# A spectral convolution with its head: the inverse transform along the rows of even layers in 32x32 tiles, and another order of work in a pair of chunks

## The chip, the cores and the metric

The kernel runs on one core of one Trainium2 chip. The metric is the device time of one execution in microseconds, the median of three runs. TensorE is called PE here, its loads of weights PEld, VectorE DVE, ScalarE ACT, GpSimd POOL, and SyncE, which only issues transfers, SP.

## The reference, cut to what matters

Eight images of 8 channels and 256 x 256 pixels. Each goes through four spectral layers (a transform of the plane, a mix of the 24 x 12 lowest frequencies, the transform back, plus a 1x1 convolution), then through a head (fc1, swish, fc2), and at the end a dilation:

```python
h = gconv1x1(concat([gn(x), grid]), fc0_w, fc0_b)          # 4 groups of 10 channels
for i in range(4):
    h1 = spectral_conv(h, sp_w1[i], sp_w2[i])               # rfft2, mix of modes, irfft2
    h2 = gconv1x1(h, w_w[i], w_b[i])
    h = h1 + h2
    if i < 3:
        h = gswish(h, betas[i])
h = gswish(gconv1x1(h, fc1_w, fc1_b), betas[3])             # 4 groups of 128 channels
x = x + gconv1x1(h, fc2_w, fc2_b)
x = x + dilate3x3(gn(x))                                    # maximum over 3 x 3 windows
```

## The kernel before

All data is fp32. Image by image, the kernel runs the four layers; the head of the image before is cut into 128 steps, which are strewn among the layers' work, and the dilation of the image before that follows in small pieces (`tail`) beside some of the steps. PE, DVE and ACT each take their instructions in the order in which the program gives them. All PSUM tiles come from one pool of four slots, each of two banks:

```python
def ps_z(name):
    return ps.tile([128, 2, 512], F32, tag="z", bufs=4, name=name)
def ps_a(name):
    return ps_z(name)[:, 0, :]
```

A layer consists of these parts. After the mix, `p_f` folds the spectrum to real sums; its result is copied to `fz`, in which the 32 values of a channel (`k`) lie on 32 columns and those of the four partition parts `q` on their own columns and partitions:

```python
p = ps_a(f"p_f_{b}_{l}")
for slot in range(2):
    for n, (table, part_of) in enumerate(((0, slot), (1 + slot, 1 - slot))):
        for q in range(4):
            mm(p[part(q), 120 * slot : 120 * slot + 120], fold[part(q), table, :],
               f[part(q), part_of]..., start=n == 0, stop=n == 1)
...
for q in range(4):
    copy(q, fz[part(q), :, :, 6 * q : 6 * q + 6]..., p[part(q), :240]...)
```

The inverse transform along the rows, `p_g`, in an even layer one matmul over the full array for each of the ten channels, then a copy to `zt`:

```python
for o in range(0, WID, 2):                      # WID = 10
    p = ps_z(f"p_g_{b}_{l}_{o}")
    for u in range(2):
        if l % 2 == 0:
            mm(p[:, u, : NBLK * CS * NQ], fz[:, o + u].rearrange("p g k -> p (g k)"),
               rowg.rearrange("p n j r -> p (n j r)"), start=True, stop=True)    # 264 columns
        else:
            ...                                  # 16 matmuls of 66 columns per channel
    for u in range(2):
        copy(u, dst, src)
    yield 0.7
```

Then eleven chunks of pixels. `burst(c)` computes the new state of a chunk (lines 476/479 and 482 on PE, two ACT instructions, line 488); `turn(c)` transposes it on DVE (line 430); `transform(k)` is the forward transform along the columns of a pair of chunks (line 447 on PE, then one half copied by DVE and the other by ACT); `gather(k)` adds it up (line 461 on PE, a DVE copy). Their order in a layer that is not the last:

```python
yield "even"                                     # a step, if needed, so that the next has an even number
for c in range(0, NCH, 2):                       # NCH = 11
    k = c // 2
    yield (1,)                                   # one step of the head, and a piece of dilation
    burst(c)
    yield (1,)
    if k > 0:
        transform(k - 1)
    late = [i for i in range(c, min(c + 2, NCH)) if i > c or c + 1 < NCH and not alone[0]]
    if c not in late:
        turn(c)
    if c + 1 < NCH:
        burst(c + 1)
    if k > 0:
        gather(k - 1)
    for i in late:
        turn(i)
out_["sw"] = [load_sw(l + 1, 0), load_sw(l + 1, 1)]
yield 1.5                                        # 1.5 shares of steps (a share is about 0.9 step)
transform(k)
yield 2
gather(k)
yield 0.5
```

`alone[0]` holds for image 0 only, beside which no head runs. A step `n` of the head is `first(n)` (fc1: line 629 on PE, two slots, two ACT instructions of line 631); after an odd step follows `second(n - 3)` (fc2 of two steps: line 651 on PE, one slot, one DVE addition of line 656):

```python
for n in range(STEPS):                           # STEPS = 128
    ...
    first(n)
    if n % 2 == 1 and n > 2:
        second(n - 3)
    yield
second(STEPS - 2)
```

Of the kernel before, what the change touches and what calls it, by code (L numbers as in the profile page):

```python
# [10 lines left out]
F32 = mybir.dt.float32  # L11
# [7 lines left out]
HW = 256  # L19
NPIX = HW * HW  # L20
G = 4
# [15 lines left out]
PIX = 2 * HW  # L37
DR = 2
STEPS = 128
SIDE = 4.2  # L40


@with_exitstack
def fno_dilate_kernel(ctx: ExitStack, tc: tile.TileContext, a: dict, out: bass.AP):
# [16 lines left out]
    def part(i):  # L61
        return slice(32 * i, 32 * i + 32)
# [30 lines left out]
    xe = load("xe", (128, 6, G, 5), nc.sync)  # L93
    wext = const.tile([128, G, WID, 5], F32, tag="c_wext", name="c_wext")
    nc.sync.dma_start(wext.rearrange("p g o j -> p (g o j)"), a["wext"].partition_broadcast(128))
    cz = load("cz", (32, 5, WID, G))
    fold = load("fold", (128, 3, 32))
    rowg = load("rowg", (128, NBLK, NQ, CS))
    binv = load("binv", (128, HW))
    eh_f = load("eh_f", (128, 3, NBLK, 32))  # L100
# [70 lines left out]
    for l in range(3):  # L171
# [4 lines left out]
    nc.vector.tensor_tensor(cz[0:1, 0], cz[0:1, 0], cv[0:1], ALU.add)  # L176
    nc.sync.dma_start(cz[25:26, 0], cv[1:2])
    nc.sync.dma_start(cz[0:1, 4], cv[2:3])
    nc.vector.tensor_tensor(
        wt, wt, io.rearrange("p (l g) -> p l g", l=4).unsqueeze(3).to_broadcast([128, 4, G, 32]), ALU.mult,  # L180
    )
# [8 lines left out]
    def copy(i, dst, src):  # L190
        if alone[0] and i % 2:
            nc.scalar.activation(dst, src, AF.Identity)  # L192
        else:
            nc.vector.tensor_copy(dst, src)  # L194
# [157 lines left out]
    def mix(b, l, out_):  # L352

        s = [sb.tile([128, 3, G, 2, WID], F32, tag=f"S{i}", bufs=1, name=f"S{i}_{b}_{l}") for i in range(2)]
        bt, sw = out_["bt"], out_["sw"]
        for k in range(3):
            for k2 in range(2):
                pr = turned[:, 2, 1024 * k2 : 1024 * k2 + 800].rearrange("p (g m i) -> p g m i", g=G, i=WID)
                nc.vector.tensor_tensor(  # L359
                    pr, sw[k], bt[:, k2, k].unsqueeze(2).to_broadcast([128, G, 2 * WID, WID]), ALU.mult)  # L360
                yield 0.7
                nc.vector.tensor_reduce(  # L362
                    s[k2][:, k].rearrange("p g s o -> p (g s o)"),
                    pr.rearrange("p g m i -> p (g m) i"), AX.X, ALU.add,
                )
                if k == 0 and k2 == 1:
                    sw.append(load_sw(l, 2))
                yield 0.7
        f = sb.tile([128, 2, 3, G, WID], F32, tag="F", bufs=1, name=f"F_{b}_{l}")
        nc.vector.tensor_tensor(f[:, 0], s[0][:, :, :, 0, :], s[1][:, :, :, 1, :], ALU.subtract)  # L370
        nc.vector.tensor_tensor(f[:, 1], s[0][:, :, :, 1, :], s[1][:, :, :, 0, :], ALU.add)
        yield 0.5

        p = ps_a(f"p_f_{b}_{l}")
        for slot in range(2):
            for n, (table, part_of) in enumerate(((0, slot), (1 + slot, 1 - slot))):
                for q in range(4):
                    mm(p[part(q), 120 * slot : 120 * slot + 120], fold[part(q), table, :],
                       f[part(q), part_of].rearrange("p k g o -> p (k g o)"), start=n == 0, stop=n == 1)
        nc.vector.tensor_copy(fz[0:32, :, :, 24], cz[:, l])  # L380
        if l == 0:
            mr = out_["mr"]
            d = sb.tile([128, 1], F32, tag="d", name=f"dm_{b}")
            nc.vector.tensor_tensor(d, mr[:, 0:1], mr[:, 1:2], ALU.mult)
            mm(p[0:1, 240 : 240 + WID * G], d, wm.rearrange("p o g -> p (o g)"), start=True, stop=True)
            nc.vector.tensor_tensor(
                fz[0:1, :, :, 24], fz[0:1, :, :, 24],
                p[0:1, 240 : 240 + WID * G].rearrange("p (o g) -> p o g", o=WID), ALU.add)
        if l < 2:
            nc.vector.tensor_copy(fz[0:32, :, :, 25], cz[:, 4 if l == 0 else 3])  # L390
        for q in range(4):
            dst = fz[part(q), :, :, 6 * q : 6 * q + 6].rearrange("p o g k -> p k g o")
            src = p[part(q), :240].rearrange("p (k g o) -> p k g o", g=G, o=WID)
            copy(q, dst, src)
        yield 2.5

    def rows_of(b, l):

        zv = zt[:, :, :, : NBLK * WID].rearrange("p r f (n o) -> p o n r f", n=NBLK)
        for o in range(0, WID, 2):  # L400
            p = ps_z(f"p_g_{b}_{l}_{o}")
            for u in range(2):
                if l % 2 == 0:
                    mm(p[:, u, : NBLK * CS * NQ], fz[:, o + u].rearrange("p g k -> p (g k)"),  # L404
                       rowg.rearrange("p n j r -> p (n j r)"), start=True, stop=True)
                else:
                    for g in range(G):
                        for j in range(NQ):
                            mm(p[part(j), u, NBLK * CS * g : NBLK * CS * (g + 1)], fz[:, o + u, g, :],  # L409
                               rowg[:, :, j, :], start=True, stop=True)  # L410
            for u in range(2):
                src = p[:, u, : NBLK * CS * NQ]
                if l % 2 == 0:
                    dst = zv[:, o + u].rearrange("p n r f -> p n f r")
                    src = src.rearrange("p (n f r) -> p n f r", n=NBLK, r=CS)
                else:
                    dst = zv[:, o + u].rearrange("p n r f -> p f n r")
                    src = src.rearrange("p (f n r) -> p f n r", f=NQ, n=NBLK)
                copy(u, dst, src)
            yield 0.7  # L420


    def layer(b, l, out_, stored, side):
        group_in_f = l % 2 == 1

        def turn(c):

            dst = turned[:, c % 3].rearrange("p (s f x) -> p f s x", s=2, f=NQ)
            for i in range(2):
                nc.vector.transpose(  # L430
                    dst[:, 2 * i : 2 * i + 2], h[:, c, 2 * i : 2 * i + 2].rearrange("p f (s x) -> p f s x", s=2))
# [67 lines left out]
        if l == 0:  # L499
# [1 line left out]
                read_x(c)  # L501
            wcn = sb.tile([128, 32], F32, tag="wcn", bufs=1, name=f"wcn_{b}")
            nc.vector.tensor_scalar(wcn, wc, out_["mr"][:, 1:2], None, ALU.mult)
        yield "even"
        if l == 3:
            room = 0.0
            for c in range(NCH):
                yield (1,)
                burst(c)
                room += SIDE  # L510
                while room > 0.0:
                    room -= next(side, SIDE)
                yield (1,)
            return
        for c in range(0, NCH, 2):
            k = c // 2
            yield (1,)
            burst(c)
            yield (1,)
            if k > 0:  # L520
                transform(k - 1)

            late = [i for i in range(c, min(c + 2, NCH)) if i > c or c + 1 < NCH and not alone[0]]
            if c not in late:
                turn(c)
            if c + 1 < NCH:
                burst(c + 1)
            if k > 0:
                gather(k - 1)
            for i in late:  # L530
                turn(i)
        out_["sw"] = [load_sw(l + 1, 0), load_sw(l + 1, 1)]
        yield 1.5
        transform(k)
        yield 2
        gather(k)
        yield 0.5

    def start(b, out_):
        if b < n_img:  # L540
# [68 lines left out]
    def head(b, stored, stats):  # L609
# [6 lines left out]
        def load_state(k):  # L616

            if k < NQ * NCH:
                j, c = k // NCH, k % NCH
                hs[k] = sb.tile([128, PIX], F32, tag="hs", bufs=4, name=f"hs_{b}_{k}")  # L620
                nc.sync.dma_start(hs[k], stored[c][:, PIX * j : PIX * (j + 1)])
# [47 lines left out]
        for n in range(STEPS):  # L669
            if n % 32 % NBLK == 0:  # L670
                load_state(n // 32 * NCH + n % 32 // NBLK + 2)
            first(n)
            if n % 2 == 1 and n > 2:
                second(n - 3)
            yield
        second(STEPS - 2)


    def dilate(b, stats):
# [5 lines left out]
        for r in range(0, 16, DR):  # L685
# [12 lines left out]
            yield  # L698
            nc.vector.tensor_tensor(m, m, yin[:, :, 2 : HW + 2], ALU.max)
            yield  # L700
            o = sb.tile([128, DR, HW], F32, tag="o", bufs=1, name=f"o_{b}_{r}")
            nc.vector.tensor_tensor(o, m[:, 0:DR], m[:, 1 : DR + 1], ALU.max)
            nc.vector.tensor_tensor(o, o, m[:, 2 : DR + 2], ALU.max)
            yield

# [83 lines left out]
def _tables():  # L789
# [50 lines left out]
    for j, v in enumerate(planes):  # L840
# [9 lines left out]
    edge[:, 2], edge[:, 3] = np.where(top, PAD, -BIG), np.where(bottom, PAD, -BIG)  # L850
    tables = {
        "fw": fw, "fw8": fw8, "stack": np.tile(np.eye(32), (4, 1)), "eh0": eh0, "eh_f": eh_f.reshape(128, 3, NBLK, 32),
        "rowg": rowg.reshape(128, NBLK, NQ, CS),
        "fold": fold.reshape(128, 3, 32), "binv": binv.reshape(128, HW),
        "xe": xe.reshape(128, 6, G, 5), "grp": grp, "edge": edge,
    }
    return {k: np.ascontiguousarray(v, f32) for k, v in tables.items()}
# [66 lines left out]
```

## Time and profile before

| | before |
|---|---|
| median of 3 runs | 4137.09 us (4132.44 to 4141.43) |
| span of the profiled run | 4130.5 us, mean granted PE clock 0.973 |
| PE busy | 3709.2 us |
| ACT busy | 2841.6 us |
| DVE busy | 2526.0 us |
| p_g of even layers on PE (line 404) | 320 records, 90.4 us |
| p_g of odd layers on PE (line 409) | 5120 records, 88.0 us |
| p_f on PE (line 378) | 1024 records, 37.4 us |

Two records of the trace stand for one fp32 matmul of the program: 160 calls of line 404 give 320. A line of groups or of the timeline names the engine, the source line, the operation, the tile written and those read, the shape, and the count; "32\*128" with a matmul is the part of the array that its weights fill (rows x columns). "Idle before" is the time for which the engine did nothing just before, with the instruction that ended this wait. In the slices of the span, each digit is the busy share in tenths of one fortieth.

### The profile page before, as it was taken

How to read it: one execution, taken by the hardware profiler on the slowest of the kernel's cores; microseconds unless marked ns; L12 is line 12 of the kernel's file. 1: busy time of each engine (PE TensorE's matmuls, PEld its weight loads, DVE VectorE, ACT ScalarE, POOL GpSimd, SP SyncE). 2: the span in 40 equal slices, each digit the busy share in tenths (PEclk: the TensorE clock that was granted, in tenths of full speed). 3: DMA queues.
4: the chain of work that ended last, by engine and by line, in shares of the span. 5: the costliest groups of instructions: out<-in, count | busy, mean ns of one | idle time of the engine just before them, and what ended most of it. 6: DMA issues, size and time to landing. Idle time of an engine off the chain costs nothing.

```text
span 4130.5 us, 118618 instructions
## 1 busy us (share of the span) xinstructions
PE 3709.2 (90%) x53530; PEld 1483.6 (36%) x53530; DVE 2526.0 (61%) x3535; ACT 2841.6 (69%) x2991; POOL 119.8 (3%) x202
## 2 busy tenths in 40 slices
PE   5666999999999999999999999999999999999997
PEld 2333333333333333333333333333333333333222
DVE  6665655556666566765666666665666656663533
ACT  3334767776667766776766776777676776678887
POOL 1000000000000000000000000000000000000000
PEclk8878999999999999999999999999999999999999
DMA  2005111331115311252122611134111432115311
GB/s 83 14 14 186 50 30 46 133 118 57 57 49 181 91 56 57 77 187 55 58 59 85 195 43 52 54 128 150 56 51 51 163 106 64 55 49 190 94 49 48
DMA packets 113984, 345.05 MB, mean 84 GB/s; under 512 B 15768, under 2 KB 18392, under 8 KB 98056
## 3 DMA queue, kind: packets, MB, share of 16 engines
q1 hardware_dynamic: 95288, 276.33, 21.6%
q0 software_dynamic: 18192, 61.13, 4.5%
q8 instruction: 422, 6.91, 0.7%
q14 instruction: 82, 0.67, 0.1%
HBM read 213.40 MB, written 123.74 MB: 82 GB/s over the span
## 4 chain that ended last, share of the span: by engine, by line
PE 74%; ACT 11%; DVE 11%; issue 3%; DMA 1%; POOL 0%; DVEq 0%; SPq 0%; POOLq 0%; ACTq 0%
PE p_fc L651 22%; PE p_fc L629 17%; PE p_z L482 8%; PE p_d L447 7%; PE p_z L479 7%; ACT act L631 5%; ACT h L488 4%; DVE turned L430 3%; PE p_b L332 2%; PE p_u L461 2%; PE p_g L409 2%; PE p_z L476 2%; PE p_g L404 2%; ACT h L490 2%; DVE fz L194 1%
## 5 line engine op out<-in xcount | busy, mean ns | idle before, releaser
L631 ACT ACTIVATE act<-p_fc 128x1024 f32<-128x1024 f32 x2048 | 1961.5, 1027 | 604.1 <-PE p_fc L629 592.5
L629 PE MATMUL p_fc<-hs,c_w 32*128 32x512 f32 x8192 | 1204.6, 629 | 30.1 <-DVE fz L194 12.8
L651 PE MATMUL p_fc<-act,c_w 128*32 128x512 f32 x8192 | 992.5, 602 | 86.0 <-ACT act L631 43.6
L656 DVE TENSOR_TENSOR y<-p_fc,y 128x512 f32<-128x512 f32 x392 | 270.4, 690 | 651.0 <-PE p_fc L651 649.2
L488 ACT ACTIVATE h<-p_z 128x1024 f32<-128x1024 f32 x528 | 511.8, 1021 | 211.6 <-PE p_z L482 211.5
L629 PEld LDWEIGHTS p_fc<-hs,c_w 32*128 32x128 f32 x8192 | 423.6, 185 | 572.5 <-ACT act L631 251.9
L430 DVE STREAM_TRANSPOSE turned<-h 128x1024 f32<-128x1024 f32 x528 | 612.6, 1213 | 14.5 <-ACT h L488 14.5
L651 PEld LDWEIGHTS p_fc<-act,c_w 128*32 128x32 f32 x8192 | 215.0, 109 | 812.5 <-issue 349.7
L482 PE MATMUL p_z<-c_binv,zt 32*128 32x256 f32 x5632 | 406.8, 401 | 0.6 <-ACT zt L192 0.6
L482 PEld LDWEIGHTS p_z<-c_binv,zt 32*128 32x128 f32 x5632 | 259.7, 184 | 301.5 <-issue 293.3
L479 PE MATMUL p_z<-h,c_wt 32*32 32x512 f32 x8448 | 355.2, 600 | 4.2 <-ACT h L488 3.5
L447 PE MATMUL p_d<-turned,c_fw 32*32 32x480 f32 (+1 forms) x9216 | 312.7, 549 | 37.9 <-DVE turned L430 36.4
L198 ACT ACTIVATE turned<-p_d 128x960 f32<-128x960 f32 x144 | 130.3, 905 | 249.6 <-PE p_d L447 249.6
L200 DVE COPY turned<-p_d 128x960 f32<-128x960 f32 x144 | 154.6, 1074 | 147.3 <-PE p_d L447 145.0
L194 DVE COPY zt<-p_g 128x264 f32<-128x264 f32 x300 | 156.0, 615 | 86.7 <-PE p_g L404 46.3
L490 ACT ACTIVATE h<-p_z,c_bias 128x1024 f32<-128x1024 f32 x176 | 186.6, 1111 | 26.1 <-PE p_z L482 25.7
L447 PEld LDWEIGHTS p_d<-turned,c_fw 32*32 32x32 f32 x9216 | 121.0, 104 | 227.8 <-issue 98.6
L362 DVE TENSOR_REDUCE S<-turned 128x80 f32<-128x800 f32 x192 | 188.9, 984 | 5.2
L359 DVE TENSOR_TENSOR turned<-t,B 128x800 f32<-128x800 f32 x192 | 188.4, 981 | 1.2 <-DMA t<-in_spw 1.0
L323 DVE STREAM_TRANSPOSE turned<-zt 128x960 f32<-128x960 f32 x96 | 174.8, 1864 | 0.8
L461 PE MATMUL p_u<-turned,c_stack 128*32 128x480 f32 (+1 forms) x1152 | 137.4, 548 | 36.3 <-DVE turned L200 36.3
L479 PEld LDWEIGHTS p_z<-h,c_wt 32*32 32x32 f32 x8448 | 97.3, 103 | 190.0 <-ACT h L488 69.1
(169 smaller groups left out, 1957.0 us busy)
## 6 DMA issues: line engine op xcount, KB each, us to landing
stored<-h SPq DMA_DIRECT2D x88, 1024.0 KB
hs<-stored SPq DMA_DIRECT2D x352, 256.0 KB
t<-in_spw SPq DMA_DIRECT2D x96, 400.0 KB
yin<-y_rows POOLq DMA_DIRECT2D x56, 512.0 KB, 5.0
h<-in_xp SPq DMA_DIRECT2D x352, 48.0 KB
turned<-in_x SPq DMA_DIRECT2D x16, 1024.0 KB
y<-in_x SPq DMA_DIRECT2D x56, 256.0 KB
y_rows<-y POOLq DMA_DIRECT2D x56, 256.0 KB, 2.3
```

The lines of the kernel that those rows point to most:

```text
L194: nc.vector.tensor_copy(dst, src)
L430: nc.vector.transpose(dst[:, 2 * i : 2 * i + 2], h[:, c, 2 * i : 2 * i + 2].rearrange("p f (s x) -> p f s x", s=2))
L447: mm(pair[q // 2][part(v % 4), q % 2, : 240 * n], fw8[part(q), v, :], t[part(q), :, :, v, : NBLK * WID], start=v < 4, stop=v >= 4)
L461: mm(p[part(g), : 240 * n], stack, m, start=True, stop=True)
L479: mm(o, wt[part(q), l, g, :], h[part(q), c, f, :], start=True, stop=False)
L482: mm(pair[q // 2][:, q % 2, HW * s : HW * (s + 1)], zt[part(q), 2 * c + s].rearrange("p f o -> p (f o)"), binv[part(q), :], start=False, s ...
L488: nc.scalar.activation(dst, pair[i], AF.Silu)
L490: nc.scalar.activation(dst, pair[i], AF.Identity, bias=bias3)
L629: mm(pair[g // 2][:, g % 2, :], w1[part(g), blk, :], hs[k][part(g), :], start=True, stop=True)
L631: nc.scalar.activation(act[:, 2 * i : 2 * i + 2, :], pair[i], AF.Silu)
L651: mm(acc[part(g), :], w2[:, g, 15 - rb - i : 47 - rb - i], act[:, g, :], start=i == 0, stop=i == 1)
L656: nc.vector.tensor_tensor(y, sums, y, ALU.add)
```

## The change

Two things change. The first is the inverse transform of even layers. The fold's table is four times as wide (its 32 columns repeated four times), so that `p_f` writes four copies of the spectrum, one on each 32 partitions; `fz` holds all four. Then a matmul of 32 rows and 32 columns suffices for one group of one channel, and the four channels of a block use the four row parts of the array and the four groups its column parts: 16 small matmuls take the place of four large ones. Odd layers go on using all 128 rows, which now add up four equal copies; so the table `rowg` is divided by 4, and in even layers `fz` is multiplied by 4. The second is the order: in a pair of chunks, of the steps beside it, at the end of a layer, and in `head`, where fc2 now stands ahead of fc1 of the next even step. Besides, the dilation writes its second maximum in place.

```diff
-        p = ps_a(f"p_f_{b}_{l}")
+        pair = [ps_z(f"p_f_{b}_{l}_{i}") for i in range(2)]
+        p = [pair[q // 2][:, q % 2, :] for q in range(4)]
...
-                    mm(p[part(q), 120 * slot : 120 * slot + 120], fold[part(q), table, :],
+                    mm(p[q][:, 120 * slot : 120 * slot + 120], fold[part(q), table, :],
...
-        nc.vector.tensor_copy(fz[0:32, :, :, 24], cz[:, l])
+        factor = 4.0 if l % 2 == 0 else 1.0
+        nc.vector.tensor_copy(fz[:, :, :, 24], cz[:, l])
         if l == 0:
...                                              # one small addition becomes four, on 1 partition each
         for q in range(4):
-            dst = fz[part(q), :, :, 6 * q : 6 * q + 6].rearrange("p o g k -> p k g o")
-            src = p[part(q), :240].rearrange("p (k g o) -> p k g o", g=G, o=WID)
-            copy(q, dst, src)
+            dst = fz[:, :, :, 6 * q : 6 * q + 6].rearrange("p o g k -> p k g o")
+            src = p[q][:, :240].rearrange("p (k g o) -> p k g o", g=G, o=WID)
+            ...                                  # the same copy, times factor
...
-        for o in range(0, WID, 2):
-            p = ps_z(f"p_g_{b}_{l}_{o}")
-            for u in range(2):
-                if l % 2 == 0:
-                    mm(p[:, u, : NBLK * CS * NQ], fz[:, o + u].rearrange("p g k -> p (g k)"), ...)
+        size = 2 if l % 2 else 4
+        for o in range(0, WID, size):
+            n = min(size, WID - o)
+            p = [ps_z(f"p_g_{b}_{l}_{o}_{i}") for i in range((n + 1) // 2)]
+            for u in range(n):
+                for g in range(G):
+                    if l % 2 == 0:
+                        mm(p[u // 2][part(g), u % 2, : NBLK * CS * NQ], fz[part(u), o + u, g, :], rows[part(u)],
+                           start=True, stop=True)
+                        continue
...
-            yield 0.7
+            yield 0.35 * n
...
-        yield "even"
         if l == 3:
+            yield "odd"
             for c in range(NCH):
-                yield (1,)
                 burst(c)
...                                              # (the transform of the next image's x, in pieces)
-                yield (1,)
+                yield (LAST,)                    # LAST = 2
             return
-        for c in range(0, NCH, 2):
...                                              # (the loop shown above)
+        yield "even"
+        for c in range(NCH):
+            k = c // 2
+            if c % 2 == 0:
+                burst(c)
+                yield (1,)
+                turn(c)
+                if k > 0:
+                    transform(k - 1)
+            else:
+                burst(c)
+                if k > 0:
+                    gather(k - 1)
+                yield (1,)
+                turn(c)
         out_["sw"] = [load_sw(l + 1, 0), load_sw(l + 1, 1)]
-        yield 1.5
+        yield 1
+        gather(k - 1)
         transform(k)
         yield 2
         gather(k)
-        yield 0.5
+        yield 1
...
+            if n % 2 == 0 and n > 3:
+                second(n - 4)
             first(n)
-            if n % 2 == 1 and n > 2:
-                second(n - 3)
             yield
+        second(STEPS - 4)
         second(STEPS - 2)
...
-            o = sb.tile([128, DR, HW], F32, tag="o", bufs=1, name=f"o_{b}_{r}")
-            nc.vector.tensor_tensor(o, m[:, 0:DR], m[:, 1 : DR + 1], ALU.max)
+            o = m[:, 0:DR]
+            nc.vector.tensor_tensor(o, o, m[:, 1 : DR + 1], ALU.max)
```

Three more transfers and three multiplications at the start of the program make the copies of the constant part (`cz`) and its factor of 4.

More of the change, by code (lines that the diff above doesn't have):

```diff
@@ L39 @@
 STEPS = 128
+LAST = 2
 SIDE = 4.2
@@ L95, in fno_dilate_kernel @@
     nc.sync.dma_start(wext.rearrange("p g o j -> p (g o j)"), a["wext"].partition_broadcast(128))
-    cz = load("cz", (32, 5, WID, G))
-    fold = load("fold", (128, 3, 32))
+    cz = const.tile([128, 5, WID, G], F32, tag="c_cz", name="c_cz")
+    nc.gpsimd.dma_start(cz[0:32], a["cz"])
+    fold = load("fold", (128, 3, 128))
     rowg = load("rowg", (128, NBLK, NQ, CS))
@@ L178, in fno_dilate_kernel @@
     nc.sync.dma_start(cz[0:1, 4], cv[2:3])
+    for l in (0, 2, 4):
+        nc.vector.tensor_scalar(cz[0:32, l], cz[0:32, l], 4.0, None, ALU.mult)
+    for q in range(1, 4):
+        nc.sync.dma_start(cz[part(q)], cz[0:32])
     nc.vector.tensor_tensor(
@@ L383, in mix @@
             d = sb.tile([128, 1], F32, tag="d", name=f"dm_{b}")
[L384 to L388, printed above, removed]
+            nc.vector.scalar_tensor_tensor(d, mr[:, 0:1], factor, mr[:, 1:2], ALU.mult, ALU.mult)
+            for q in range(4):
+                mm(p[0][32 * q : 32 * q + 1, 240 : 240 + WID * G], d, wm.rearrange("p o g -> p (o g)"),
+                   start=True, stop=True)
+            for q in range(4):
+                row = slice(32 * q, 32 * q + 1)
+                nc.vector.tensor_tensor(
+                    fz[row, :, :, 24], fz[row, :, :, 24],
+                    p[0][row, 240 : 240 + WID * G].rearrange("p (o g) -> p o g", o=WID), ALU.add)
         if l < 2:
-            nc.vector.tensor_copy(fz[0:32, :, :, 25], cz[:, 4 if l == 0 else 3])
+            nc.vector.tensor_copy(fz[:, :, :, 25], cz[:, 4 if l == 0 else 3])
         for q in range(4):
-            dst = fz[part(q), :, :, 6 * q : 6 * q + 6].rearrange("p o g k -> p k g o")
-            src = p[part(q), :240].rearrange("p (k g o) -> p k g o", g=G, o=WID)
-            copy(q, dst, src)
+            dst = fz[:, :, :, 6 * q : 6 * q + 6].rearrange("p o g k -> p k g o")
+            src = p[q][:, :240].rearrange("p (k g o) -> p k g o", g=G, o=WID)
+            if alone[0] and q % 2:
+                nc.scalar.activation(dst, src, AF.Identity, scale=factor)
+            else:
+                nc.vector.tensor_scalar(dst, src, factor, None, ALU.mult)
         yield 2.5
@@ L399, in rows_of @@
         zv = zt[:, :, :, : NBLK * WID].rearrange("p r f (n o) -> p o n r f", n=NBLK)
-        for o in range(0, WID, 2):
-            p = ps_z(f"p_g_{b}_{l}_{o}")
-            for u in range(2):
-                if l % 2 == 0:
[L404 to L412, printed above, removed]
+        rows = rowg.rearrange("p n j r -> p (n j r)")
+        size = 2 if l % 2 else 4
[6 more added lines that the diff above has]
+                        mm(p[u // 2][part(g), u % 2, : NBLK * CS * NQ], fz[part(u), o + u, g, :], rows[part(u)],
+                           start=True, stop=True)
+                        continue
+                    for j in range(NQ):
+                        mm(p[0][part(j), u, NBLK * CS * g : NBLK * CS * (g + 1)], fz[:, o + u, g, :],
+                           rowg[:, :, j, :], start=True, stop=True)
+            for u in range(n):
+                src = p[u // 2][:, u % 2, : NBLK * CS * NQ]
                 if l % 2 == 0:
@@ L512, in layer @@
                     room -= next(side, SIDE)
-                yield (1,)
-            return
-        for c in range(0, NCH, 2):
-            k = c // 2
-            yield (1,)
[L518 to L524, printed above, removed]
-                turn(c)
[L526 to L531, printed above, removed]
+                yield (LAST,)
+            return
+        yield "even"
[3 more added lines that the diff above has]
+                burst(c)
+                yield (1,)
+                turn(c)
+                if k > 0:
+                    transform(k - 1)
+            else:
+                burst(c)
[3 more added lines that the diff above has]
+                turn(c)
         out_["sw"] = [load_sw(l + 1, 0), load_sw(l + 1, 1)]
-        yield 1.5
+        yield 1
+        gather(k - 1)
         transform(k)
@@ L852, in _tables @@
         "fw": fw, "fw8": fw8, "stack": np.tile(np.eye(32), (4, 1)), "eh0": eh0, "eh_f": eh_f.reshape(128, 3, NBLK, 32),
-        "rowg": rowg.reshape(128, NBLK, NQ, CS),
-        "fold": fold.reshape(128, 3, 32), "binv": binv.reshape(128, HW),
+        "rowg": rowg.reshape(128, NBLK, NQ, CS) / 4.0,
+        "fold": np.tile(fold.reshape(128, 3, 32), (1, 1, 4)), "binv": binv.reshape(128, HW),
         "xe": xe.reshape(128, 6, G, 5), "grp": grp, "edge": edge,
```

## The prediction

> **What bounds the kernel now.** I read the busy shares and the forty slices first, then the stretch of one image, then PE's own order of blocks inside it.
>
> From the page, the shares and the slices (tenths busy; PEclk is the granted clock):
> ```profile
> PE 3709.2 (90%) x53530; PEld 1483.6 (36%) x53530; DVE 2526.0 (61%) x3535; ACT 2841.6 (69%) x2991; POOL 119.8 (3%) x202
> ...
> PE   5666999999999999999999999999999999999997
> ```
> PE is the bound, except in the first four slices (image 0 alone, before any head runs beside it). Busy time by windows gives the periods: 0 to 389 us is image 0, then seven periods of 493 us (in 880 to 1373 PE is busy 460.5, ACT 351.8, DVE 318.1), then 290 us in which the last head runs alone. So a period is PE's work plus about 33 us of PE waiting, and what counts is time on PE's queue, seven times.
>
> I write B for a burst (p_z), F for one step of fc1, S for fc2 of two steps, T for the transform (p_d), U for the gather (p_u). The timeline of PE over one pair of chunks (start, length, line; in brackets the idle time before):
> ```profile
> 1535.30 1.14 PE L479 MATMUL p_z<-h,c_wt 32*32 32x512 f32 x32
> 1536.37 1.16 PE L482 MATMUL p_z<-c_binv,zt 32*128 32x256 f32 x16
> 1537.34 1.05 PE L629 MATMUL p_fc<-hs,c_w 32*128 32x512 f32 x8
> 1538.62 1.93 PE L651 MATMUL p_fc<-act,c_w 128*32 128x512 f32 x16 [0.24 <-ACT h L488]
> 1540.48 2.19 PE L447 MATMUL p_d<-turned,c_fw 32*32 32x480 f32 x61
> ...
> 1543.71 1.15 PE L482 MATMUL p_z<-c_binv,zt 32*128 32x256 f32 x16
> 1544.78 1.01 PE L461 MATMUL p_u<-turned,c_stack 128*32 128x480 f32 x8
> 1545.73 1.36 PE L629 MATMUL p_fc<-hs,c_w 32*128 32x512 f32 x8
> ```
> The next pair starts at 1547.02: 11.72 us, with one visible wait of 0.24. From start to start: F 1.29 behind U; B's two halves 1.07 and 0.97 (1.08 if U follows); F with the wait 1.28; S 1.86; T with the next half burst 3.23; U 0.95. ACT works 8.6 us in this stretch, DVE 8.2 (busy time by windows), so neither bounds it.
>
> The inverse transform along the rows of an even layer (p_g, line 404), same view:
> ```profile
> 1630.44 2.05 PE L404 MATMUL p_g<-c_rowg,fz 128*128 128x264 f32 x8
> 1632.42 1.14 PE L629 MATMUL p_fc<-hs,c_w 32*128 32x512 f32 x8
> 1633.49 2.05 PE L404 MATMUL p_g<-c_rowg,fz 128*128 128x264 f32 x8
> 1635.47 1.30 PE L629 MATMUL p_fc<-hs,c_w 32*128 32x512 f32 x8
> 1636.70 1.92 PE L651 MATMUL p_fc<-act,c_w 128*32 128x512 f32 x16
> 1638.56 1.16 PE L404 MATMUL p_g<-c_rowg,fz 128*128 128x264 f32 x4
> ```
> No wait here: the stage is all PE. Eight records (four channels, two records per call) hold the queue for 1.98 us, four for 1.09.
>
> The end of an even layer, and PE's waits over one period (1370 to 1863 us: total, times, longest):
> ```profile
> 1448.82 2.24 PE L447 MATMUL p_d<-turned,c_fw 32*32 32x480 f32 x64
> 1452.40 1.01 PE L461 MATMUL p_u<-turned,c_stack 128*32 128x480 f32 x8 [1.34 <-DVE turned L200]
> 1454.68 2.24 PE L447 MATMUL p_d<-turned,c_fw 32*32 32x240 f32 x64 [1.26 <-DVE turned L430]
> ```
> ```profile
> PE p_u L461 <- DVE turned L200: 4.3, 3, 1.7
> ...
> PE p_d L447 <- DVE turned L430: 2.5, 2, 1.3
> ```
> Nothing else runs on PE there, so U waits for the copy out of T, and T for the last transposes: 6.8 us in a period.
>
> [...] 64 records of 480 columns in T take 549 ns each and finish within 2.24 us. [...] here 32x32 takes 104 ns, 32x128 185 and 128x128 202. [...] the burst's second half holds the queue 0.97 us before F (same mode) and 1.08 before U (another), so about 0.1 a change. [...]
>
> **The change, part by part** (per period, unless said).
>
> 1. Inverse transform, two even layers. A record of 264 columns lasts 386 ns, one of 66 columns 220: 0.84 ns a column, and 0.165 fixed. Now: layer 2 takes 1.98 + 1.98 + 1.09 = 5.05 us, and F or FF behind a full-array block is some 0.16 longer (1.23 for 1.07), twice: 5.4. After: four channels are 32 records on 16 tiles, two rounds of 264 x 0.84 = 0.22 us, so 0.44. The burst's 32x32 half (32 records of 512 columns, ideal 0.86) takes 1.07, so I add 0.21: 0.65. A second floor: 128 records of the odd p_g leave in 1.98 us, 15.5 ns each, so 32 need 0.5. I take 0.7, and 0.65 for the last two channels: 2.05. New wait: after the change two slots fill at once and DVE empties four channels in 1.98 us. The order of the built program has the first two groups apart by two steps or by F S S (no wait), but the last group behind one F of 1.07, while its slot is emptied only after some 1.3: 0.3. Gain 5.4 - 2.35 = 3.1 a layer, **6.2**.
>
> 2. Four copies of the spectrum. p_f keeps 32 records, with weights of 128 columns instead of 32 (load 185 ns for 104). Eight rounds of 0.10 us have to hide longer loads: I guess 0.3 more each, four times. It takes two slots for one, so FF behind it waits a little longer (now 0.58 to 0.78). In layer 0 three more small additions of 0.21 stand before DVE's copies. Sum **-2.0**. The copies themselves are as long as before: 240 elements, only on 128 partitions.
>
> 3. Order in a pair: now F B F S T B U, after B S F T B U F. The PE blocks, from the durations above: B 1.07 + 1.08, S 1.85, F 1.07, T with half burst 3.23, B 1.08, U 0.94, F 1.29: 11.61, as the 0.24 wait goes but one more change of mode comes. Against it: DVE's order puts the two transposes of chunk c (2.36 us) ahead of the copy out of T. With B's start as zero, S ends at 4.0, its addition at 4.85, a piece of dilation (0 to 1.55, mean 0.9) follows, then 2.36, then the copy 1.16: 8.4 to 9.9. U could start at 9.4. Mean wait 0.3; and the second burst needs the slots that ACT frees from F at about 7.2, when T hands over. I take 11.95, 0.23 more than now, in 12 pairs: **-2.8**. Layer 3's cycle (B F S F) is the same sequence of blocks as now.
>
> 4. End of a layer: the transposes of chunk 10 move ahead of T, so the 1.26 wait goes; but the copy out of T waits behind them. In layers 0 and 2 no step falls between that T and U: wait 2.1 for 2.6 and 2.9; in layer 1 about 1.1 for 1.34. **+1.5**.
>
> Period: 6.2 - 2.0 - 2.8 + 1.5 = 2.9 us, seven times 20. Image 0: its even p_g takes 6.34 us at the lower clock, but DVE and ACT copy ten times 0.62 in turn, so 0.5 at most per layer; at each layer's end T now runs beside the transposes, 1.3 three times; p_f costs 2. Together +3. The last 290 us have the same F F S cycle. The in-place dilation saves memory, not instructions. Total about 23: 4137 becomes **4114**.
>
> **Rivals.** (a) PE bound, no new waits: then the full 6.8 of part 1, order neutral, end waits gone: 10 us a period, 4060. For it: PE is 93% busy and every PE block is on the path. Against: the slots. (b) The new order waits: if U always stands behind DVE, or B behind ACT, 0.6 more per pair is 50 us over seven periods, which eats the whole gain: 4140 to 4160. For it: the present order has DVE free when T ends (copy starts 2.28 us after T's start), the new one has not. (c) The 32x32 tiles do not overlap when four of one row group follow one another (T and B step through the row groups first): then p_g takes up to 4 x 0.44 and nothing is won: 4150.
>
> **Range and chances.** The middle is the sum; (a) and (b) are the ends, each about as likely. 4068 to 4150. For over 2% it would have to fall below 4054, past what (a) gives: 0.08. Over 2% slower would need 4220: 0.03.
>
> **What would show it.** p_g on PE in an even layer: 0.65 to 0.7 per four channels (right) or near 2 (c). The pair: start to start 11.95, with a wait of U on DVE's copy. Layer's end: a wait of U near 2 and none of T. p_f 1.3 for 1.0. Wrong if the pair is off by more than 0.4 either way, since it comes 84 times and more, or if waits for slots show up in the stage of p_g.

## The result, and the profile after

The kernel after takes **4064.87 us** (median of four runs, 4060.59 to 4067.95), the kernel before, on the same chip, 4138.54. The ratio is 0.9823, with a 95% interval of 0.9806 to 0.9840: 74 us were gained, where 23 had been predicted, and the time lies just below the range (4068). In the two profiled executions the spans are 4130.5 and 4063.3 us. Of these 67.2 us, 9.3 are gained in image 0 (the first fc1 on PE starts at 383.66 for 392.99), 53.4 in the seven periods, and 4.5 behind the last burst.

The page after, the shares:
```profile
PE 3730.1 (92%) x54538; PEld 1439.2 (35%) x54538; DVE 2528.0 (62%) x3562; ACT 2852.1 (70%) x2991; POOL 117.0 (3%) x202
```
PE is the bound as before. It is busy for *longer* (3730 for 3709 us), so what was gained is waiting. PE's waits over the whole run say which (total us, times, longest). First before, then after:
```profile
PE p_f L378 <- DVE F L370: 71.7, 24, 13.0
...
PE p_d L447 <- DVE turned L430: 36.4, 32, 1.4
PE p_u L461 <- DVE turned L200: 36.3, 27, 1.7
PE p_fc L651 <- ACT h L488: 30.0, 105, 1.7
...
PE p_fc L629 <- ACT act L631: 4.1, 7, 0.6
```
```profile
PE p_f L386 <- DVE F L377: 46.9, 4, 13.2
PE p_u L481 <- DVE turned L207: 42.9, 51, 2.4
...
PE p_fc L647 <- ACT act L649: 16.4, 33, 0.6
...
PE p_d L467 <- DVE turned L450: 11.0, 14, 1.4
```
The wait of `p_f` for DVE's mix fell from 24 times to the four of image 0. The prediction had not spoken of it. T's wait for the transposes fell by 25 us, as the prediction's part 4 had it for the periods, and U's grew by 7. The wait of fc1 for the slots that ACT frees is 12 us larger. The 30 us for which S waited behind a burst (`h L488`) are gone as well, but the bursts themselves hold PE's queue 5.2 us a period longer, so that is no gain. The `p_f` wait is thus the first suspect for the error.

For the working below I divided PE's queue over five steady periods by kinds of block, from start to next start less the idle time shown. A period is 493.5 us before and 484.6 after. Per period (us; "act" is ACT's swish behind fc1):

| | before | after | order alone (experiment 2) |
|---|---|---|---|
| `p_g` of the even layers | 10.3 | 4.3 | 10.5 |
| fc1 | 149.3 | 150.4 | 147.0 |
| `p_f` | 4.1 | 5.6 | 4.0 |
| all waits shown | 31.3 | 20.8 | 16.8 |
| of them: `p_f` on DVE's mix / on act | 3.55 / 2.07 | 0 / 1.42 | 0 / 0.56 |
| fc1 on DVE's copies out of `p_f` / on act | 1.93 / 0.59 | 0 / 2.48 | 0 / 0.60 |
| T on transposes, U on the copy | 2.52, 4.33 | 0, 5.42 | 0, 5.42 |
| period | 493.5 | 484.6 | 483.1 |

After, fc2 and no longer fc1 waits for the copies out of `p_f`, 0.5 us. The last column already holds the surprise: with the old `p_f` and `p_g`, the period is shorter still.

### The profile page after: what moved, and what is told of

Read it like the earlier page. It is cut to its first block, busy times and chain, and to the rows that moved or that the text cites. A ratio compares the mean times of both kernels' runs of the same rounds, so it can differ in the third digit from the quotient of the medians.

```text
span 4063.3 us, 120753 instructions
## 1 busy us (share of the span) xinstructions
PE 3730.1 (92%) x54538; PEld 1439.2 (35%) x54538; DVE 2528.0 (62%) x3562; ACT 2852.1 (70%) x2991; POOL 117.0 (3%) x202
## 4 chain that ended last, share of the span: by engine, by line
PE 76%; DVE 11%; ACT 8%; issue 4%; DMA 1%; POOL 0%; DVEq 0%; POOLq 0%; SPq 0%; ACTq 0%
PE p_fc L669 22%; PE p_fc L647 20%; PE p_z L502 8%; PE p_z L499 7%; PE p_d L467 6%; ACT act L649 5%; PE p_u L481 3%; PE p_z L496 2%; DVE turned L450 2%; PE p_b L339 2%; PE p_g L429 2%; ACT h L510 2%; DVE turned L330 1%; DVE turned L207 1%; PE p_f L386 1%
## 5 line engine op out<-in xcount | busy, mean ns | idle before, releaser
L647 PE MATMUL p_fc<-hs,c_w 32*128 32x512 f32 x8192 | 1229.5, 632 | 27.0 <-ACT act L649 16.4
L669 PE MATMUL p_fc<-act,c_w 128*32 128x512 f32 x8192 | 1002.8, 604 | 49.8 <-ACT act L649 35.5
L647 PEld LDWEIGHTS p_fc<-hs,c_w 32*128 32x128 f32 x8192 | 407.8, 184 | 735.2 <-ACT act L649 324.4
L450 DVE STREAM_TRANSPOSE turned<-h 128x1024 f32<-128x1024 f32 x528 | 623.2, 1219 | 26.7 <-ACT h L508 26.4
L669 PEld LDWEIGHTS p_fc<-act,c_w 128*32 128x32 f32 x8192 | 228.7, 110 | 654.1 <-issue 355.7
L499 PE MATMUL p_z<-h,c_wt 32*32 32x512 f32 x8448 | 371.2, 603 | 6.8 <-DVE y L674 3.7
L467 PEld LDWEIGHTS p_d<-turned,c_fw 32*32 32x32 f32 x9216 | 121.7, 103 | 186.9 <-issue 150.4
L481 PE MATMUL p_u<-turned,c_stack 128*32 128x480 f32 (+1 forms) x1152 | 136.9, 545 | 42.9 <-DVE turned L207 42.9
L207 DVE COPY turned<-p_d 128x960 f32<-128x960 f32 x144 | 152.1, 1056 | 29.2 <-PE p_d L467 29.1
```

Of the source, the lines that this page charges most:

```text
L450: nc.vector.transpose(dst[:, 2 * i : 2 * i + 2], h[:, c, 2 * i : 2 * i + 2].rearrange("p f (s x) -> p f s x", s=2))
L467: mm(pair[q // 2][part(v % 4), q % 2, : 240 * n], fw8[part(q), v, :], t[part(q), :, :, v, : NBLK * WID], start=v < 4, stop=v >= 4)
L481: mm(p[part(g), : 240 * n], stack, m, start=True, stop=True)
L499: mm(o, wt[part(q), l, g, :], h[part(q), c, f, :], start=True, stop=False)
L647: mm(pair[g // 2][:, g % 2, :], w1[part(g), blk, :], hs[k][part(g), :], start=True, stop=True)
L669: mm(acc[part(g), :], w2[:, g, 15 - rb - i : 47 - rb - i], act[:, g, :], start=i == 0, stop=i == 1)
```

## The experiments

All times are medians; the ratios are to the kernel before, run on the same chip. F, S, B, T, U stand for the blocks as in the prediction.

**1 and 2: the two halves of the change.** The first keeps the old order and takes the four copies, the 32x32 `p_g` and the dilation in place. The second keeps the old `p_f`, `p_g` and dilation and takes the new order.
```diff
# 1, on the kernel before: size 4, fold on 128 columns, factor 4, o = m[:, 0:DR]; loops and head as before
# 2, on the kernel after:
-        pair = [ps_z(f"p_f_{b}_{l}_{i}") for i in range(2)]
+        p = ps_a(f"p_f_{b}_{l}")
-        size = 2 if l % 2 else 4      # and the 32x32 matmuls
+        for o in range(0, WID, 2):    # one full-array matmul per channel
```


> The kernel before, with the inverse transform of even layers in 32x32 tiles and the four copies of the spectrum, but with the old order everywhere. If the transform gives what its blocks show (p_g 6.0 us less per period on PE, p_f 1.5 more) and no wait changes, the time is 4138 - 7 x 4.5 = 4107. If the four slots taken at once cost waits, it is 4120 or more. If the transform carries the whole gain and the order gives nothing, it is 4065 to 4075.

Measured: 4126.13, ratio 0.9959 (0.9943 to 0.9975).

> The kernel after, with the inverse transform and p_f as they were before: only the order is changed. The prediction on record had the order as a small loss (2.8 lost in the pairs, 1.5 won at the layers' ends, per period): then 4145. If the rest of the measured gain (8.9 - 4.5 = 4.4 us per period) belongs to the order, 4138 - 31 = 4107.

Measured: 4047.60, ratio 0.9773 (0.9759 to 0.9788). The first fell on its second branch (4120 or more): `p_g` holds the queue 5.4 us a period less, but PE's waits rise from 31.3 to 33.1. The second missed by 60 us. The small tiles with their four copies are worth 15 us with the old order. The order alone is worth 93, more than the whole change: with the new order, the tiles and copies together *cost* 17 us.

**3: where the order gains.** The kernel before, with one step of the head moved from behind `p_f` to the place between DVE's sums and `p_f`:
```diff
-        yield 0.5        # behind the sums F, ahead of p_f
+        yield 1.5
-        yield 2.5        # behind the copies out of p_f
+        yield 1.5
```


> The kernel before, with one share of the head's steps moved from behind p_f to ahead of it (yield 0.5 to 1.5 ahead, 2.5 to 1.5 behind). Theory: a good part of the gain is that p_f no longer waits for the mix on DVE, since in the new order one more step stands ahead of it; then PE's waits at p_f (5.6 us per period) go to about 1, and the time is 4138 - 7 x 4 = 4110. Rival: the wait only moves (p_g then waits for the copies of p_f, as fewer steps lie between): 4130 to 4140.

Measured: 4084.51, ratio 0.9865 (0.9850 to 0.9879), more than expected. This edit touches neither the pairs nor `p_g`, and gives 56 us by the medians (44 between the two profiled executions, 6.2 a period). The trace shows what it removes. The timeline of PE and DVE before, ahead of `p_f` in layer 1:
```profile
1490.01 1.92 PE L651 MATMUL p_fc<-act,c_w 128*32 128x512 f32 x16 [0.15 <-ACT act L631]
1492.01 0.69 DVE L656 TENSOR_TENSOR y<-p_fc,y 128x512 f32<-128x512 f32 x1 [0.52 <-PE p_fc L651]
1492.61 0.27 DVE L370 TENSOR_TENSOR F<-S,S 128x120 f32<-128x120 f32 x1
1493.03 1.02 PE L378 MATMUL p_f<-F,c_fold 32*32 32x120 f32 x32 [1.09 <-DVE F L370]
```
Between S and `p_f` PE has nothing. DVE has ended the mix's products and stands idle for S (0.52; 1.86 in layer 0), since the addition of S's result stands ahead of the two sums `F` that `p_f` reads. So in layers 0 and 1 (waits of 1.09). In layer 3 S stands last too, but DVE works on the mix until the addition starts, so of the wait of 1.37 the addition (0.60 from its start to the sum's) is a part only. In layer 2 a step of fc1 lies between, but also a product and a reduction of the mix, and the wait is 2.07. The profile puts that one down to ACT's emptying of fc1, which ends 0.03 us before `p_f` starts; but `p_f` starts 0.15 us after the first sum ends, as in the other layers, so the mix is likelier. Then fc1 behind `p_f` waits 0.58 to 0.79 for DVE's copies, in three layers. The kernel after, PE, layer 2:
```profile
1584.64 1.92 PE L669 MATMUL p_fc<-act,c_w 128*32 128x512 f32 x16 [0.28 <-ACT act L649]
1586.50 1.14 PE L647 MATMUL p_fc<-hs,c_w 32*128 32x512 f32 x8
1587.66 1.17 PE L386 MATMUL p_f<-F,c_fold 32*128 32x120 f32 x32
```
Here DVE's addition (1586.64) and the sums (1587.25, 1587.44) lie beside an fc1. The head now issues S ahead of F in an even step, so a step never ends with S: in all four layers at least one fc1 falls between S and `p_f`. In experiment 3 an fc1 falls between in two layers, and in the two others the sums stand ahead of that addition. One new wait takes part of it back: `p_g` of the even layers then waits 1.6 a period for the copies out of `p_f`.

**4: is it the place or the number of steps?** The kernel after has 8, 8, 8, 8 steps ahead of `p_f` in the layers' mix, where before had 7, 8, 8, 7. Here it gets fewer, 8, 7, 7, 7:
```diff
-                yield 0.7        # twice in the mix
+                yield 0.64
-        yield 2.5                # behind p_f
+        yield 3.22
```


> The kernel after, with one step of the head moved from ahead of p_f to behind it in layers 1 to 3 (the mix's yields 0.7 to 0.64, 2.5 to 3.22 behind p_f). If the freedom of p_f from waiting is part of the gain, its wait comes back with some 1 to 2 us in each of three layers: 4065 + 7 x 4 = 4093. If not, 4065.

Measured: 4057.77, ratio 0.9799 (0.9783 to 0.9816): not slower but, if anything, a little faster. The waits on the mix come back (0.30 in one layer and 1.18 in another, where a product and a reduction fall behind the addition), but those for `p_f`'s two slots (0.28 + 0.43 in each of two layers of the kernel after) go. The number of steps is not what carried the gain.

**11: the head's order without the loop's.** The kernel before with S ahead of F in the even steps, the chunk loop as it was:
```diff
+            if n % 2 == 0 and n > 3:
+                second(n - 4)
             first(n)
-            if n % 2 == 1 and n > 2:
-                second(n - 3)
             yield
+        second(STEPS - 4)
         second(STEPS - 2)
```


> The kernel before with fc2 of two steps ahead of fc1 of the next even step (the new head), all else old. Theory: p_f's wait depends on where fc2's addition falls on DVE among the last products of the mix: if fc2 stands at the end of an odd step, its addition holds DVE up just before the mix ends. Then p_f's waits (5.6 us per period) mostly go, as they did in the new order, though as many steps or fewer stand ahead of it: 4138 - 30 = 4108. If only one more step ahead of p_f helps, as tried before, this stays within 10 us of 4138.

Measured: **4288.26**, ratio 1.0361 (1.0345 to 1.0376), a clear miss. The sum of `p_f`'s waits did fall, from 5.6 to 3.1 a period. But in a pair the blocks now follow as S F B F T B U, and a pair takes 13.5 us for 11.7. PE's timeline in such a pair:
```profile
971.65 1.05 PE L476 MATMUL p_z<-h,wcn 6*32 6x512 f32 x4
972.89 1.14 PE L476 MATMUL p_z<-h,wcn 6*32 6x512 f32 x28 [0.19 <-ACT act L631]
```
F, B, F and T each want slots, and no S (one slot, 1.86 us) stands between to let ACT catch up: B stops after 4 records for a slot, and T waits 0.25 for ACT before it starts. The new head thus goes with the new loop, which puts B S F T and keeps the pair at 11.8 (below). No run has the new loop with the old head.

**5, 8: the small tiles with one slot at a time.** The kernel after with two channels at once:
```diff
-        size = 2 if l % 2 else 4
+        size = 2
```


> The kernel after, with two channels to a block in even layers too (8 tiles of 32x32, one slot of the pool for two). PE's own work at p_g grows a little (five blocks of about 0.6 us for 0.77 + 0.77 + 0.67). Theory: what the small tiles save comes back as waiting, as four channels take two of the four slots and the next step of fc1 must wait until ACT has emptied the one before (F behind p_g holds the queue 1.97 us plus a wait of 0.47, for 1.07). With one slot the second tile of fc1 alone has to wait: F behind p_g about 1.5, no wait at its start, and the time falls below that of the order alone: 4040. Rival: the extra time of F comes from the small tiles themselves (change of mode, loads of weights); then five blocks instead of three make it worse: 4070 to 4080.

Measured: 4060.91, ratio 0.9809 (0.9796 to 0.9822); 4040 had been expected. Taking two slots at once is thus at most a small part of the loss. (In the kernel after each of the four channels has half a slot to itself; whether they could share, no run shows.) The timeline of PE in layer 2 shows where the tiles' saving goes. Kernel after, then experiment 2 with the full array:
```profile
1592.63 1.14 PE L647 MATMUL p_fc<-hs,c_w 32*128 32x512 f32 x8
1593.71 0.77 PE L425 MATMUL p_g<-c_rowg,fz 32*32 32x264 f32 x32
1594.95 2.04 PE L647 MATMUL p_fc<-hs,c_w 32*128 32x512 f32 x8 [0.47 <-ACT act L649]
1596.92 1.92 PE L669 MATMUL p_fc<-act,c_w 128*32 128x512 f32 x16
```
```profile
1596.12 1.14 PE L628 MATMUL p_fc<-hs,c_w 32*128 32x512 f32 x8
1597.19 2.05 PE L405 MATMUL p_g<-c_rowg,fz 128*128 128x264 f32 x8
1599.17 1.30 PE L628 MATMUL p_fc<-hs,c_w 32*128 32x512 f32 x8
1600.41 1.16 PE L405 MATMUL p_g<-c_rowg,fz 128*128 128x264 f32 x4
```
`p_g` is 1.3 us shorter, yet from F's start to the end of the second F it takes 1596.92 - 1592.63 = **4.29** us with the small tiles, and 1600.41 - 1596.12 = **4.29** with the full array. The second F stands for the slots that ACT empties behind the first: it waits 0.47, and then its 8 records spread over 1.97 us for 1.24. With two channels at once the same stretch is 3.36 us, and 3.37 in the full array.

**9, 10: the same with half of ACT's work.** If ACT's swish is the limit behind that equality, the small tiles must win once it is halved. In both kernels the swish is left out on the right 256 of 512 columns, and fc2 reads the left half twice, so PE's work is as before and the output is not the reference's. 9 is the order alone, 10 the kernel after.
```diff
-                nc.scalar.activation(act[:, 2 * i : 2 * i + 2, :], pair[i], AF.Silu)
+                nc.scalar.activation(act[:, 2 * i : 2 * i + 2, :], pair[i][:, :, :256], AF.Silu)
-                    mm(acc[part(g), :], w2[...], act[:, g, :], ...)
+                    mm(acc[part(g), :], w2[...], act[:, g, :].unsqueeze(1).to_broadcast([128, 2, 256]), ...)
```


> The order alone (full-array p_g), but ACT computes the swish of only the left half of the columns of fc1, and fc2 reads that half twice: PE and DVE do the same work, each of ACT's two instructions behind fc1 is half as long, and the output is not the reference's. Taken for the comparison with the next run. It is faster than 4048 by whatever PE waited for ACT's emptying of fc1: 4000 to 4035.

> The same half swish in the kernel after (32x32 p_g), with the same loss of output. Theory: the 6 us per period that p_g lost on PE came back as waiting of the next fc1 for ACT, since a step of fc1 frees its slots only some 3.1 us after it starts. With ACT at half length the slots come free about a microsecond earlier, so the small tiles pay: this run is faster than the one before it by 15 to 30 us, where with the full swish it is slower by 17. Rival: the small tiles' block costs PE its time in another way (change of mode, loads); then it stays slower than the one before, by about 10.

Measured: 9 takes 3973.85 (0.9599, 0.9583 to 0.9615), faster than expected; 10 takes 3948.76 (0.9542, 0.9526 to 0.9558), 25 us less, as expected. With the full swish the tiles and copies cost 17 us, with half of it they gain 25. The stretch F, four channels, F is now 4.12 us in 9 (1571.06 to 1575.18) and 3.42 in 10 (1561.79 to 1565.21). Its last two blocks, 9 and then 10:
```profile
1572.13 2.05 PE L405 MATMUL p_g<-c_rowg,fz 128*128 128x264 f32 x8
1574.11 1.14 PE L628 MATMUL p_fc<-hs,c_w 32*128 32x512 f32 x8
```
```profile
1562.86 0.77 PE L425 MATMUL p_g<-c_rowg,fz 32*32 32x264 f32 x32
1563.67 1.61 PE L647 MATMUL p_fc<-hs,c_w 32*128 32x512 f32 x8
```

An equal stretch is not yet a loss, so I took whole stages of these four kernels, in which the same steps of the head fall (waits included, means of five periods, us a period; two stretches of the kernel after with the clock at half, told of below, are left out):

| | order alone (2) | after | 9 | 10 |
|---|---|---|---|---|
| end of the block ahead of `p_f` to the first `p_g`, four layers | 21.4 | 25.0 | 21.0 | 22.3 |
| first `p_g` to the first burst, even layers | 29.2 | 28.0 | 28.6 | 24.5 |
| the same, odd layers | 29.8 | 30.6 | 29.2 | 29.4 |

At `p_g` the small tiles do win, but only 1.3 us of the 6.2 that the block got shorter. What loses is the four copies: 3.5 us at `p_f`, and 0.8 more in the odd layers. Behind `p_f` in layer 2, kernel after and then order alone:
```profile
1588.81 2.04 PE L647 MATMUL p_fc<-hs,c_w 32*128 32x512 f32 x8
```
```profile
1586.71 1.32 PE L628 MATMUL p_fc<-hs,c_w 32*128 32x512 f32 x8
```
With half the swish `p_g` wins 4.1 and the copies cost 1.4, so ACT's emptying of slots sets much of both. The three stages give 3.1 us a period against the change; without the clock's part, the periods differ by 3.2, so the dilation in place has no share that shows. No run has the four copies with the full-array `p_g`.

**6, 7: the end of a layer.** U waits there, since `yield 1` gives no step between T and U in layers 0 and 2. Experiment 6 is experiment 2 with a step that always comes; 7 is experiment 3 with the new end of a layer; 8 is experiment 5 with the edit of 6.
```diff
# 6 and 8
-        yield 1
+        yield (1,)
         gather(k - 1)
# 7: turn(c) ahead of the last transform(k - 1), then
-        yield 1.5
+        yield 1
+        gather(k - 1)
         transform(k)
```


> The order alone (full-array p_g), with one step fixed between the transform of the last pair but one and its gather in every layer (yield 1 becomes yield (1,)). There PE waits 1.3, 0.3 and 2.4 us in the three layers for the copy on DVE that stands behind the transposes of chunk 10. A step of 1.07 between takes most of two of these waits: 2.5 us per period less, 4048 - 18 = 4030. If the piece of dilation that comes with a fixed step stands in DVE's way, nothing is won: 4048.

> The kernel before with p_f one share later and the new order at the end of a layer, the old order in the pairs and in the head. Of the 10.4 us per period that the order alone gives, p_f's place gave 6.2. If the layer's end gives the 2.5 us of the transform's wait, this is 4084 - 18 = 4066, and 2 us per period are left for the pairs. If the copy behind the transposes costs as much, 4084.

> Both edits, two channels to a block and the fixed step at the layer's end, on the kernel after. If they add, 4022; if the gain of either is only a shift of the steps, no better than the better one.

Measured: 6 takes **4022.15** (0.9714, 0.9701 to 0.9727), 7 takes 4107.36 (0.9923, 0.9909 to 0.9936), 8 takes 4040.98 (0.9762, 0.9749 to 0.9776). 6 is the best version: it beats the kernel after by 43 us and experiment 2 by 25. Its line in the list of PE's waits, to be held against 42.9 in the kernel after:
```profile
PE p_u L462 <- DVE turned L201: 24.5, 56, 1.7
```
8 missed its 4022 and is 19 us slower than 6: the small tiles and the copies cost as much here as between experiment 2 and the kernel after. 7 missed badly; it is 23 us slower than experiment 3. There U waits 7.1 a period for DVE, for 4.3 before, and 2.1 more for ACT, while T's 2.5 are gone. Of the 3.9 a period between 3 and 7, 2.1 are clock (7.2 lost for 5.1; see the last section).

## Why the prediction was wrong, point by point

**What failed first: a term that the sum did not have.** The prediction read the waits of U and T in the list of PE's waits, but left out the line of `p_f` on DVE that stood between others in the same list (3.6 us, and 2.1 more on ACT). The 1.9 of fc1 behind `p_f` it expected to grow a little. Waits of `p_f` and of fc1 on DVE's copies together fell from 7.55 to 1.42 us a period, and to 0.56 with the order alone. Experiment 3 takes the same three from 7.55 to 0.89 by another edit, pays 1.6 at `p_g`, and gains 6.2 a period. So the prediction had the order as a loss of 1.3 a period (parts 3 and 4), and it gained 10.4: 7.0 from these waits, 2.8 at the layers' ends, 0.8 lost in the pairs, the rest below. It had the tiles and copies as a gain of 4.2, and they cost 1.5, or 3.2 without the clock's part. Two errors of 11.7 and 5.7 with opposite signs make the one of 6.0 a period that the total shows.

**Part 1, the gain of 6.2, was mis-sized by what comes back.** The block itself came as predicted: 0.77 us shown for four channels and 0.67 for two, 6.0 us a period freed (10.3 to 4.3), so that rival (c) is out. The prediction's new wait was for DVE's emptying of `p_g`. The real one was ACT's, of fc1's slots: against the order alone, each of the four F behind four channels holds the queue some 0.74 us longer and waits 0.47 more, 4.8 of the 6.2 that `p_g` is shorter there. Of the gain 1.3 is left (2.1 with the old order). A wait for slots in the stage of `p_g` was one of the prediction's own signs of being wrong. The reasoning "No wait here: the stage is all PE" was the fault: with ACT's full work, a second F as short as 1.24 us stood there only because the full-array `p_g` in front of it gave ACT the time.

**Part 2, "-2.0",** was too small in the new order: the stage of `p_f` is 3.5 longer than with the order alone. `p_f` holds the queue 1.6 longer and waits 0.9 more for its slots, fc2 waits 0.5 for the copies, and F behind it takes 0.5 more; 0.8 in the odd layers' `p_g` come on top. With the old order the copies cost nothing there (36.5 us for the stage in experiment 1 and before, the clock's part left out): PE stood for the mix anyway. Together with part 1: 1.3 - 3.5 - 0.8 = -3.0 against the order alone (3.1 before rounding). The periods differ by only 484.6 - 483.1 = 1.5, as the clock lost 1.7 less.

**Part 3, "11.95 ... -2.8", failed.** From one T to the next the mean of the twelve pairs is 11.79 us for 11.73, the median 11.64 for 11.72. The first bursts of two pairs on PE's timeline:
```profile
1504.78 1.18 PE L499 MATMUL p_z<-h,c_wt 32*32 32x512 f32 x32
...
1516.44 1.18 PE L499 MATMUL p_z<-h,c_wt 32*32 32x512 f32 x32
```
They are 11.66 us apart, with no wait between. The sum of blocks, 11.61, was right. What was added to it, a mean wait of 0.3 of U for DVE, is rare: it shows in four of the twelve pairs, 0.18 to 0.70, 1.4 a period. The wait of 0.24 ahead of S did go, but the bursts hold the queue longer by about as much. The 0.1 that the sum counts for a change of mode shows in the trace as a difference between neighbours: between 1400 and 2300 us of the kernel after, a burst's second half (32\*128 of the array) holds the queue 0.97 us with an fc1 (32\*128) behind it and 1.08 with S (128\*32), medians of 16 and 31. What happens in it is not shown.

**Part 4, "+1.5",** held in kind and was too small: T's 2.52 went, and U's three waits at the ends fell from 4.3 to 4.05, together +2.8 (the 5.42 of the table has the pairs' 1.4 in it). At the end of layer 2:
```profile
1671.57 2.24 PE L467 MATMUL p_d<-turned,c_fw 32*32 32x480 f32 x64
1676.26 1.01 PE L481 MATMUL p_u<-turned,c_stack 128*32 128x480 f32 x8 [2.44 <-DVE turned L207]
```
U waits 2.44 (the three layers: 1.34, 0.27, 2.44; about 2.1, 1.1, 2.1 had been said), the second T not at all.

**Image 0, "+3",** gained 9.3. T's wait for the transposes is 7.8 us less up to the first fc1.

**A reading.** The 549 ns that the prediction gives for T's records of 480 columns is the mean over those and the 240-column ones; the 480-column records alone take 571. Nothing in the sum rests on it: that 32x32 tiles work side by side shows with either, as 64 such records end within 2.24 us, and after, 32 records of `p_g`, of 440 ns in the mean, within 0.77. That sixteen do, as part 1's two rounds have it, was an estimate. The 104, 185 and 202 ns are the mean lengths of one load of weights on PEld.

**The rivals.** (a) named nearly the right time, 4060, for a wrong reason: it had no new waits and the full 6.8 of part 1. (b) was wrong: the new order was the gain. Its danger is real, though, as experiment 11 shows, but on the side of ACT's slots and not of DVE.

**What stays open.** Of the order's 10.4 a period, 0.3 are clock and 1.1 are not assigned; of the whole change's 8.9, 2 are clock, told of below, and no experiment separates that. That fc2's addition is what DVE stands for at `p_f` in layers 0 and 1 is read from the timelines and fits experiments 3 and 4; no run moved that addition alone.

## What to carry to other kernels

A block that got shorter on the bounding engine is a gain only if the block behind it can start: measure the stretch from one user of a buffer to the next, here 4.29 us with either `p_g`, and not the block. Measure also the stage that prepares its data: the copies at `p_f` cost more than the tiles won. Before predicting, list *every* wait of the bounding engine and ask of each what the new order puts in front of it; a DVE addition that depends on the last block of a step is hidden if another block follows that doesn't need it (here the 3.55 us a period for which `p_f` waited for the mix on DVE went to 0). And an order comes whole: the head's part of this one, by itself, made the kernel 3.6% slower.

## What was not expected of the hardware

PE's clock falls to half for some 3.5 us in the midst of a busy stretch. The kernel after, busy time by windows (PE, PEld, DVE, ACT, POOL, then the granted clock, the DMA share and GB/s):
```profile
1603.70:1607.20 3.50, 3.50 (x21) 0.57 (x16) 1.08 (x2) 0.56 (x1) 0.00 (x0) 0.51 0.40 131
```
In it the S of 16 records takes 3.61 us for 1.92, and no wait is shown: it looks like work. The longest gap shown in the ten microseconds before, in which the granted clock is 1.00, is 0.47, and the F behind it hides some 0.7 more among its records, so in these ten microseconds PE makes no long pause. Summed over the period, the time lost (length by one less the clock) is 3.75 us before, 1.7 after, 3.4 with the order alone, and 7.2 in experiment 7 (mean granted clocks of the profiled runs 0.973, 0.975, 0.975 and 0.969); a difference of 2 us a period between two kernels can therefore be clock. It need not be apart from the order, though. Of the eleven such stretches in the five periods before, eight begin within 1.3 us of the end of waits of 2 to 3 us in all, of `p_f` (2.07) or of U and T at a layer's end, which the new order shortens or removes; the three others begin within 2.6 us of one of 0.53. After, there are five. That the waits bring the stretches on is not shown.
